# A four-direction selective scan between layer norm and FFN: padded middle-group weights, one load per quad of rows, other places for the pieces, and four products of a step on GpSimd

## The chip, the core and the metric

The kernel runs on one core of a Trainium2 chip. The metric is the device time of one execution in microseconds (us), the median of three runs. The engines of the core work side by side, each through its own instructions in order: TensorE (PE, matmuls; PEld is its weight load), VectorE (DVE), ScalarE (ACT), GpSimd (POOL), and SyncE (SP), whose queue issues the DMA transfers here. SBUF is the on-chip memory of 128 partitions, PSUM the memory that PE writes.

## What is computed

Two images of 96 channels and 128 x 128 pixels go through two layers. Layer 0 adds a state-space mixer (Mamba) over four scan directions to its input, then a quantized feed-forward network; layer 1 adds a 3 x 3 convolution and another feed-forward network. Nearly all the time goes into the mixer. Cut to what matters, for each direction:

```
xz = x @ in_w.T;  xc, z = split(xz)                 # 192 channels each
xc = silu(causal_conv_of_4_taps(xc) + conv_b)
dt_raw, B, C = split(xc @ xproj_w.T)                # 6, 16 and 16 columns
dt = softplus(dt_raw @ dt_w.T + dt_b)
for t in time:                                      # 16384 positions
    h = exp(dt[t] * A) * h + dt[t] * B[t] * xc[t]   # 192 channels x 16 states
    y[t] = sum over states of h * C[t]
out = (y + D * xc) * silu(z) @ outp_w.T
```

The four directions are row-major, its reverse, column-major and its reverse; their outputs are joined by one more matrix and added to the input.

## The kernel before

**Tiling.** For each image the kernel normalizes (`normalize`), runs the mixer (`mamba`), then the rest (`ffn_and_conv`). The mixer takes the directions in two pairs (`PAIRS`): row-major with column-major, then the two reverses. The 2 x 192 channels of a pair fill three groups (g) of 128 partitions: group 0 belongs to the first direction, group 2 to the second, and the middle group 1 has 64 channels of each, the first direction in partitions 0 to 63. Time is cut into 32 tiles of 512 positions; a pair and a tile make a *step*, 64 per image. A step has 24 *units*: a group and two of the 16 states (s, s + 1), so units 0 to 7 are group 0, 8 to 15 the middle group, 16 to 23 group 2.

**One unit.** ACT computes the two decays exp(dt * A) into a PSUM tile `da` (`decay`, L330; three buffers). POOL multiplies dt * u with the rows of B, in place in the row tile (`b_part`, L324). DVE runs two scans (`scan`, L334), which read da and b and leave the states h in da, and multiplies h with the rows of C into c (`behind`, L409, [128, 1024]). ACT saves the last states to `hst` (L410). PE adds the two halves of c into the PSUM tile `y` by identity matmuls (`sums`, L341); y starts with the D * xc term (`dmat`, L416). After the last unit of a group DVE multiplies y with the gate (`gated`, L349), and `project` and `collect` (L357, L359, L365) bring a step's groups into the image.

**Rows.** The rows of B and C of a step are computed on PE (L251), copied by ACT (`rows_out`, L258), written to DRAM four times over (`bcd`, L261), and read back with every partition getting the same 4 states x 512 positions (`row_tile`, L320). Such a *quad* serves two units. Groups 0 and 2 load it in one DMA of 1024 KB; the middle group, whose halves belong to two directions, takes two of 512 KB. B has four buffers of quads, C three.

**Order.** The order on PE, ACT, DVE, POOL and SP is the program's, written out by hand. The main loop over k, one unit each, issues: the B load of unit k + 6 (when k is even), `b_part` of unit k + 2, the pieces with (k, 0), the first scan of k, `behind(k - 1)`, the second scan of k, the C load of unit k + 4 (when k is even), the decay of k + 2, and the pieces with (k, 1). The *pieces* belong to the next step and are placed at units of the current one (`prologue`, its list `at`): the load of xa and xb, the input convolution of each group with its output copy (`conv`, `conv_out`), the gate (`gate`, `gate_out`), the silu of both (each with two loads of ACT's function table), the rows, and the softplus of dt in seven parts (`dt_in` to `dt_u`) for each group. All pieces share one PSUM bank, `misc`, so a piece's matmul waits until ACT has read the last one's result.

**What the change touches.** `inproj` (L197 to L208) writes the middle group as two matmuls of 64 columns each, one per direction, to the two halves of the bank. `BY_POOL` is empty in this kernel, so `by_pool` (L343) does not run: it would make a unit's product on POOL, with the states left in b.

Of the kernel before, what the change touches and what calls it, by code (L numbers as in the profile page):

```python
# [10 lines left out]
F32 = mybir.dt.float32  # L11
# [22 lines left out]
B_AHEAD = 3  # L34
C_AHEAD = 2
AHEAD = 2
BY_POOL = ()
BCO = 32
NBC = 4 * S

# [2 lines left out]
def tile_metaformer(ctx: ExitStack, tc: tile.TileContext, a: dict, out: bass.AP):  # L43
# [22 lines left out]
    inz = const("inz", (C, 4, DI))  # L66
# [11 lines left out]
    inx = cpool.tile([C, 4, 4, DI], F32, name="inx")  # L78
    nc.vector.memset(gmat, 0.0)
    with tc.tile_pool(name="prep", bufs=1) as pp, tc.tile_pool(name="prep_ps", bufs=2, space=PSUM) as pps:  # L80
        alog = pp.tile([128, 2, NG, S], F32, name="alog")
        nc.sync.dma_start(alog, a["alog"])
        nc.scalar.activation(alog, alog, AF.Exp)
        nc.vector.tensor_scalar_mul(amat, alog, -1.0)

        dskip = pp.tile([128, 2, NG], F32, name="dskip")
        nc.sync.dma_start(dskip, a["dskip"])
        for pi in range(2):
            for g in range(NG):
                nc.vector.tensor_scalar_mul(dmat[:, pi, g, :], ident, dskip[:, pi, g : g + 1])  # L90

        inxw = pp.tile([C, 4, DI], F32, name="inxw")
        nc.sync.dma_start(inxw, a["inx"])
        taps = pp.tile([C, 4, 4, DI], F32, name="taps")
        nc.sync.dma_start(taps, a["taps"].broadcast_to((C, 4, 4, DI)))
        for d in range(4):
            nc.vector.tensor_tensor(inx[:, d], taps[:, d], inxw[:, d, None, :].broadcast_to((C, 4, DI)), ALU.mult)
        outw = pp.tile([C, 4, DI], F32, name="outw")
        nc.sync.dma_start(outw, a["outw"])
        fusew = pp.tile([C, 4, C], F32, name="fusew")  # L100
        nc.sync.dma_start(fusew, a["fusew"])
        for pi, (da, db) in enumerate(PAIRS):

            pieces = [
                (slice(0, 128), da, 0, 128),
                (slice(0, 64), da, 128, 192),
                (slice(64, 128), db, 0, 64),
                (slice(0, 128), db, 64, 192),
            ]
            for g, (rows, d, lo, hi) in enumerate(pieces):  # L110
                ps = pps.tile([128, C], F32, name="ps")
                nc.tensor.matmul(ps[rows, :], outw[:, d, lo:hi], fusew[:, d, :], start=True, stop=True)
                nc.vector.tensor_copy(gmat[rows, pi, g, :], ps[rows, :])

    def layernorm(x, eps, dst, wp, psp, bufs=2, **cast):

# [66 lines left out]
    def mamba(acc, xnr, xnc):  # L183

        with ExitStack() as st:
# [8 lines left out]
            def misc():  # L194
                return ps_m.tile([128, T], F32, name="misc")

            def inproj(pi, g, w, src, taps):  # L197

                ps = misc()
                for k in taps:  # L200
                    se = {"start": k == taps[0], "stop": k == taps[-1]}
                    for d, rows, lo, hi in (
                        ((0, slice(0, 128), 0, 128),),
                        ((0, slice(0, 64), 128, 192), (1, slice(64, 128), 0, 64)),
                        ((1, slice(0, 128), 64, 192),),
                    )[g]:
                        nc.tensor.matmul(ps[rows, :], w(PAIRS[pi][d], k, lo, hi), src[d][:, k : k + T], **se)  # L207
                return ps  # L208

            def prologue(pi, i, d):  # L210
# [14 lines left out]
                    d["dt"], d["dtu"], d["yg"] = [], [], []  # L225

                def conv(g):
                    d["ps"] = inproj(pi, g, lambda dd, k, lo, hi: inx[:, dd, k, lo:hi], src, (0, 1, 2, 3))

                def conv_out(g):  # L230
                    if g == 0:
# [1 line left out]
                    nc.scalar.activation(d["xc"][:, g, :], d["ps"], AF.Identity, bias=convb[:, pi, g : g + 1])  # L233

                def gate(g):
                    d["ps"] = inproj(pi, g, lambda dd, k, lo, hi: inz[:, dd, lo:hi], src, (3,))

                def gate_out(g):
                    if g == 0:
# [13 lines left out]
                        )  # L253

                def rows_out():

                    d["rows"] = one.tile([BCO + NBC, T], F32, name="rows")
                    nc.scalar.copy(d["rows"], d["ps"][0 : BCO + NBC, :])  # L258
                    d["bcd"] = rows_d.tile([COPIES, 2, NBC // 2, T], F32, name="bcd")
                    for n in range(COPIES):  # L260
                        nc.sync.dma_start(d["bcd"][n].rearrange("k r t -> (k r) t"), d["rows"][BCO:, :])  # L261

# [35 lines left out]
                    d["dtu"].append(dtu)  # L298


                at = [(0, 0, load), (8, 1, partial(silu, "xc")), (14, 1, partial(silu, "sz"))]
                at += [(12, 0, rows), (12, 1, rows_out)]
                for g, k in enumerate((4, 5, 6)):
                    at += [(k, 0, partial(conv, g)), (k, 1, partial(conv_out, g))]
                for g, k in enumerate((7, 10, 11)):
                    at += [(k, 0, partial(gate, g)), (k, 1, partial(gate_out, g))]
                for g, k in enumerate((13, 18, 21)):
                    pieces = (0, 0, dt_in), (0, 1, dt_exp), (1, 1, dt_ln), (2, 0, dt_q), (3, 0, dt_log), (3, 0, dt_sum), (4, 0, dt_u)
                    at += [(k + m, where, partial(f, g)) for m, where, f in pieces]
# [12 lines left out]

            def b_part(d, g, b):
# [15 lines left out]
            def sums(s, y, c):  # L339
                for j in range(2):  # L340
                    nc.tensor.matmul(y, ident, c[:, j, :], start=False, stop=s + j == S - 1)  # L341
# [61 lines left out]
            def behind(k):  # L403

                n, u = divmod(k, nu)
                (pi, i), d, (g, s) = steps[n], state[n], units[u]
                h, c = hs.pop(k), cs.pop(k)
                if (g, s) not in BY_POOL:
                    nc.vector.tensor_tensor(c, h, c, ALU.mult)  # L409
                nc.scalar.copy(hst[:, g, s : s + 2], h[:, :, T - 1])  # L410
# [155 lines left out]
def _layout(v):  # L566

    f = np.float32
    order = [d for pair in PAIRS for d in pair]
    rows = lambda w: w[order].reshape(2, NG, 128, -1).transpose(2, 0, 1, 3)  # L570
# [11 lines left out]
    grouped = lambda w: w.reshape(2, NG, 128, -1).transpose(2, 0, 1, 3)  # L582
    out = {
        "x": v["x"].reshape(NB, C, L),
        "ident": np.eye(128, dtype=f),
        "inx": v["L0_conv_in_w"][:, :DI].transpose(2, 0, 1),
        "inz": v["L0_conv_in_w"][:, DI:].transpose(2, 0, 1),
        "taps": v["L0_conv_conv_w"].transpose(0, 2, 1)[None],
        "convb": rows(v["L0_conv_conv_b"])[..., 0],
        "bcw": grouped(bcw),  # L590
        "dtw": dtw,
        "dtb": rows(v["L0_conv_dt_b"])[..., 0],
        "alog": rows(v["L0_conv_A_log"]),
        "dskip": rows(v["L0_conv_Dp"])[..., 0],
        "outw": v["L0_conv_outp_w"].transpose(1, 0, 2),
        "fusew": v["L0_conv_fuse_w"].reshape(C, 4, C).transpose(2, 1, 0),
        "fuseb": v["L0_conv_fuse_b"].reshape(C, 1),
        "kw": v["L1_conv_kernel"].transpose(1, 2, 3, 0).reshape(C, 9, C),
# [24 lines left out]
```

## Time and profile before

| | us |
|---|---|
| median of 3 runs | 13006.98 |
| lowest, highest | 13003.53, 13008.28 |
| the profiled execution | 13004.29 |
| its span, first to last instruction | 13002.5 |

The page's columns for a group of instructions are: line, engine, operation, output and inputs, shape and number; then busy time in us and the mean of one in ns; then the idle time of the engine just before them and what ended it. A window's row gives its length, the busy time of each engine in it, PE's granted clock, the busy share of the DMA engines and what they moved. In the timeline a row is a start, a length, an engine, a line, an operation, and in brackets the idle time before it and its releaser.

The two mixers fill most of the span, the first from about 168 us to 5936 us, the second from about 6660 us to 12427 us (first scans and last gate products of the timeline). A 5200 us stretch inside the first, 600 to 5800 us, shows the shares there:

| engine | busy us of 5200 |
|---|---|
| DVE | 4946.10 |
| PE | 4358.69 |
| POOL | 4071.97 |
| ACT | 3502.99 |
| DMA share, GB/s | 0.92, 289 |

DMA issues: 2048 row loads of 1024 KB (7.5 us to landing), 2048 of 512 KB (8.0 us), 512 row writes of 128 KB (9.8 us).

### The profile page before, as it was taken

To read this page: it belongs to the slowest core of one execution; us is meant where nothing else is said; L and a number is where in the kernel's file an instruction comes from. 1 tells how busy PE (TensorE), PEld (TensorE's weight loads), DVE (VectorE), ACT (ScalarE), POOL (GpSimd) and SP (SyncE) were. 2 spreads that over 40 slices of the span, in tenths; PEclk is the share of its full clock that TensorE was granted. 3 is DMA by queue.
4 is the path that set the end of the run, shared out by engine and by line. 5 is a ranking of instruction groups with operands and counts; after the bars stand their busy time and mean duration, and the time that the engine had idled before them with its cause. 6 is when DMAs were issued, how large, how long until landed. Compare 5 with 4: busy or idle time off the path is not lost. (4 is left out here: it accounts for less than half of the span.)

```text
span 13002.5 us, 97992 instructions
## 1 busy us (share of the span) xinstructions
PE 10850.3 (83%) x24208; PEld 3987.1 (31%) x24208; DVE 11569.1 (89%) x10865; ACT 8560.0 (66%) x14738; POOL 9215.4 (71%) x4772
## 2 busy tenths in 40 slices
PE   6888888888888888888978888888888888888889
PEld 2323233333333333333323333332333333333233
DVE  5999999999999999995459999999999999999954
ACT  6666666666666666665566666666666666666655
POOL 4877778777787787772147778777787777877721
PEclk8999999999999999999989999999999999999999
DMA  7999999999999999992079999999999999999920
GB/s 226 287 294 282 298 288 285 295 283 298 288 285 295 283 295 289 285 295 68 13 226 285 298 283 292 290 285 298 285 291 291 284 298 286 290 294 281 296 61 13
DMA packets 545331, 3400.40 MB, mean 262 GB/s; under 512 B 81612, under 2 KB 82732, under 8 KB 146840
## 3 DMA queue, kind: packets, MB, share of 16 engines
q1 hardware_dynamic: 544760, 3394.12, 83.1%
q8 instruction: 195, 3.19, 0.1%
q14 instruction: 376, 3.08, 0.1%
HBM read 3288.94 MB, written 104.86 MB: 261 GB/s over the span
## 5 line engine op out<-in xcount | busy, mean ns | idle before, releaser
L324 POOL TENSOR_TENSOR row<-dtu,row 128x1024 f32<-128x1024 f32 x3072 | 7175.7, 2358 | 1739.3 <-DMA row<-bcd 1419.2
L334 DVE TENSOR_TENSOR_SCAN da<-da,hst,row 128x512 f32<-128x512 f32 x5952 | 7339.4, 1274 | 351.2 <-ACT da L330 194.6
L341 PE MATMUL y<-row,ident 128*128 128x512 f32 x12288 | 6120.1, 626 | 1113.3 <-DVE row L409 1098.9
L330 ACT ACTIVATE da<-dt,amat 128x512 f32<-128x512 f32 x6144 | 4249.4, 692 | 207.5 <-ACT hst L410 0.4
L341 PEld LDWEIGHTS y<-row,ident 128*128 128x128 f32 x12288 | 2288.9, 197 | 4779.4 <-DVE row L409 2292.3
L409 DVE TENSOR_TENSOR row<-da,row 128x1024 f32<-128x1024 f32 x3072 | 3705.9, 1206 | 19.6 <-DMA row<-bcd 18.8
L410 ACT COPY hst<-da 128x2 f32<-128x2 f32 x3072 | 484.0, 158 | 2235.5 <-DVE row L409 2233.3
L416 PE MATMUL y<-xc,dmat 128*128 128x512 f32 x768 | 526.1, 773 | 779.1 <-DVE sz L349 779.1
L287 POOL TENSOR_TENSOR q<-e,q 128x512 f32<-128x512 f32 x384 | 488.0, 1271 | 821.8 <-ACT hst L410 709.1
L233 ACT ACTIVATE xc<-misc,convb 128x512 f32<-128x512 f32 x384 | 264.2, 688 | 1117.5 <-PE misc L207 1117.5
L207 PE MATMUL misc<-xa,inx 96*128 96x512 f32 (+1 forms) x2048 | 932.4, 597 | 59.0 <-DMA xa<-xnr 57.2
L207 PE MATMUL misc<-xb,inx 96*64 96x512 f32 (+1 forms) x2048 | 928.1, 595 | 1.6 <-ACT xc L233 1.6
L531 POOL TENSOR_TENSOR acc<-acc,y 96x512 f32<-96x512 f32 x128 | 147.6, 1153 | 987.0 <-DVE y L530 987.0
L541 PE MATMUL pc<-pad,kw 96*96 96x512 f32 x1152 | 566.7, 593 | 0.0
L207 PEld LDWEIGHTS misc<-xa,inx 96*128 96x128 f32 (+1 forms) x2048 | 323.6, 163 | 625.5 <-issue 493.4
L293 POOL TENSOR_TENSOR dt<-dt,ln 128x512 f32<-128x512 f32 x384 | 486.9, 1268 | 30.1
L297 POOL TENSOR_TENSOR dtu<-dt,xc 128x512 f32<-128x512 f32 x384 | 488.5, 1272 | 0.5
L290 POOL TENSOR_TENSOR ln<-ln,q 128x512 f32<-128x512 f32 x384 | 488.1, 1271 | 0.5
L359 PE MATMUL misc<-sz,gmat 128*96 128x512 f32 x1024 | 483.6, 594 | 0.0
L416 PEld LDWEIGHTS y<-xc,dmat 128*128 128x128 f32 x768 | 129.0, 211 | 1102.1 <-DVE sz L349 1099.1
L268 PE MATMUL misc<-rows,dtw 12*128 12x512 f32 x768 | 439.7, 652 | 18.5 <-ACT dt L275 17.2
L132 DVE TENSOR_TENSOR xq<-xm,rs 96x512 fp8e5<-96x512 f32 x128 | 87.9, 687 | 387.8 <-ACT rs L128 387.8
(75 smaller groups left out, 8403.8 us busy)
## 6 DMA issues: line engine op xcount, KB each, us to landing
row<-bcd SPq DMA_DIRECT2D x2048, 1024.0 KB, 7.5
row<-bcd SPq DMA_DIRECT2D x2048, 512.0 KB, 8.0
bcd<-rows SPq DMA_DIRECT2D x512, 128.0 KB, 9.8
xa<-xnr SPq DMA_DIRECT2D x124, 193.1 KB, 5.8
xb<-xnc SPq DMA_DIRECT2D x124, 193.1 KB, 5.5
acc<-in_x_dram SPq DMA_DIRECT2D x16, 768.0 KB, 17.8
xnr<-xn SPq DMA_DIRECT2D x16, 768.0 KB, 4.3
xnc<-stg SPq DMA_DIRECT2D x16, 768.0 KB, 5.6
```

What stands on the lines that cost most here:

```text
L207: nc.tensor.matmul(ps[rows, :], w(PAIRS[pi][d], k, lo, hi), src[d][:, k : k + T], **se)
L287: nc.gpsimd.tensor_tensor(d["q"], d["e"], d["q"], ALU.subtract)
L290: nc.gpsimd.tensor_tensor(d["ln"], d["ln"], d["q"], ALU.add)
L293: nc.gpsimd.tensor_tensor(d["dt"][g], d["dt"][g], d["ln"], ALU.add)
L297: nc.gpsimd.tensor_tensor(dtu, d["dt"][g], d["xc"][:, g, :], ALU.mult)
L324: nc.gpsimd.tensor_tensor(b, d["dtu"][g][:, None, :].broadcast_to((128, 2, T)), b, ALU.mult)
L330: nc.scalar.activation(da[:, j, :], d["dt"][g], AF.Exp, scale=amat[:, pi, g, s + j : s + j + 1])
L334: nc.vector.tensor_tensor_scan(h[:, j, :], da[:, j, :], b[:, j, :], 0.0 if i == 0 else hst[:, g, s + j : s + j + 1], ALU.mult, ALU.add,)
L341: nc.tensor.matmul(y, ident, c[:, j, :], start=False, stop=s + j == S - 1)
L409: nc.vector.tensor_tensor(c, h, c, ALU.mult)
L416: nc.tensor.matmul(y, dmat[:, pi, g, :], d["xc"][:, g, :], start=True, stop=False)
L541: nc.tensor.matmul(pc, kw[:, t, :], rows, start=t == 0, stop=t == 8)
```

## The change

1. **Padded weights.** The in-projection's weights of the middle group are laid out on the host as two [96, 128] blocks, one per direction, with zeros in the other direction's columns. `inproj` adds them in one accumulation of 128 columns. The output weights are padded likewise.
2. **Rows in turn.** The middle group's channels of the two directions alternate by partition (the host permutes every array that has these channels), so its quad is one DMA of 1024 KB. The rows are written to DRAM by two DMAs, each with a broadcast source, in place of four.
3. **Pieces at other units**, and each output copy or dt part in the following half.
4. **Products on GpSimd.** Units with (g, s) = (0, 4), (0, 8), (1, 4), (1, 8), which are 2, 4, 10 and 12 of a step, have their states written over b and their product with C made on POOL; their sums on PE are issued two units later.
5. The taps' weights are prepared in four parts through one buffer.

```diff
-BY_POOL = ()
+BY_POOL = ((0, 4), (0, 8), (1, 4), (1, 8))
...
-            def inproj(pi, g, w, src, taps):
+            def inproj(g, w, src, taps):
 
                 ps = misc()
-                for k in taps:
-                    se = {"start": k == taps[0], "stop": k == taps[-1]}
-                    for d, rows, lo, hi in (
-                        ((0, slice(0, 128), 0, 128),),
-                        ((0, slice(0, 64), 128, 192), (1, slice(64, 128), 0, 64)),
-                        ((1, slice(0, 128), 64, 192),),
-                    )[g]:
-                        nc.tensor.matmul(ps[rows, :], w(PAIRS[pi][d], k, lo, hi), src[d][:, k : k + T], **se)
+                parts = [(k, j) for k in taps for j in ((0,), (1, 2), (3,))[g]]
+                for n, (k, j) in enumerate(parts):
+                    nc.tensor.matmul(ps, w(k, j), src[j // 2][:, k : k + T], start=n == 0, stop=n == len(parts) - 1)
                 return ps
...
                 def rows_out():
-
                     d["rows"] = one.tile([BCO + NBC, T], F32, name="rows")
                     nc.scalar.copy(d["rows"], d["ps"][0 : BCO + NBC, :])
-                    d["bcd"] = rows_d.tile([COPIES, 2, NBC // 2, T], F32, name="bcd")
-                    for n in range(COPIES):
-                        nc.sync.dma_start(d["bcd"][n].rearrange("k r t -> (k r) t"), d["rows"][BCO:, :])
+
+                def rows_to_dram():
+
+                    d["bcd"] = rows_d.tile([2, COPIES, NBC // 2, T], F32, name="bcd")
+                    for k in range(2):
+                        r = d["rows"][BCO + k * NBC // 2 : BCO + (k + 1) * NBC // 2, None, :]
+                        r = r.broadcast_to((NBC // 2, COPIES, T))
+                        nc.sync.dma_start(d["bcd"][k].rearrange("n r t -> r n t"), r)
...
-                at = [(0, 0, load), (8, 1, partial(silu, "xc")), (14, 1, partial(silu, "sz"))]
-                at += [(12, 0, rows), (12, 1, rows_out)]
-                for g, k in enumerate((4, 5, 6)):
-                    at += [(k, 0, partial(conv, g)), (k, 1, partial(conv_out, g))]
-                for g, k in enumerate((7, 10, 11)):
-                    at += [(k, 0, partial(gate, g)), (k, 1, partial(gate_out, g))]
-                for g, k in enumerate((13, 18, 21)):
-                    pieces = (0, 0, dt_in), (0, 1, dt_exp), (1, 1, dt_ln), (2, 0, dt_q), (3, 0, dt_log), (3, 0, dt_sum), (4, 0, dt_u)
+                at = [(0, 0, load), (7, 1, partial(silu, "xc")), (12, 1, partial(silu, "sz"))]
+                at += [(12, 1, rows), (13, 0, rows_out), (13, 1, rows_to_dram)]
+                for g, k in enumerate((2, 4, 6)):
+                    at += [(k, 0, partial(conv, g)), (k + 1, 0, partial(conv_out, g))]
+                for g, k in enumerate((9, 10, 11)):
+                    at += [(k, 1, partial(gate, g)), (k + 1, 0, partial(gate_out, g))]
+                for g, k in enumerate((14, 17, 20)):
+                    pieces = (0, 1, dt_in), (1, 0, dt_exp), (1, 1, dt_ln), (3, 0, dt_q), (4, 0, dt_log), (4, 0, dt_sum), (5, 0, dt_u)
                     at += [(k + m, where, partial(f, g)) for m, where, f in pieces]
...
                 t = gen.tile([128, 4, T], F32, name=f"row{k}", bufs=ahead + 1)
-                for half in range(2) if g == 1 else (slice(None),):
-                    rows = slice(half * 64, half * 64 + 64) if g == 1 else half
-                    at = s + S * (half if g == 1 else g // 2)
-                    n = (64 if g == 1 else 128) // COPIES
-                    src = d["bcd"][None, :, k, at : at + 4, :].broadcast_to((n, COPIES, 4, T))
-                    nc.sync.dma_start(t[rows], src)
+
+                rows, nd = d["bcd"][k].rearrange("n (d s) t -> n d s t", d=2)[:, :, s : s + 4, :], 2
+                if g != 1:
+                    rows, nd = rows[:, g // 2 : g // 2 + 1], 1
+                src = rows.rearrange("n d s t -> (n d) s t")[None].broadcast_to((128 // nd // COPIES, nd * COPIES, 4, T))
+                nc.sync.dma_start(t, src)
                 return t
...
-            def by_pool(s, y, h, c):
+            def by_pool(h, c):
                 nc.gpsimd.tensor_tensor(c, h, c, ALU.mult)
-                sums(s, y, c)
...
-                    later(k + 1, 1, by_pool, s, y, h, c)
+                    later(k + 1, 1, by_pool, h, c)
+                    later(k + 3, 1, sums, s, y, c)
...
-        taps = pp.tile([C, 4, 4, DI], F32, name="taps")
-        nc.sync.dma_start(taps, a["taps"].broadcast_to((C, 4, 4, DI)))
-        for d in range(4):
-            nc.vector.tensor_tensor(inx[:, d], taps[:, d], inxw[:, d, None, :].broadcast_to((C, 4, DI)), ALU.mult)
+        for k in range(4):
+            taps = pp.tile([C, 2, NG + 1, 128], F32, name="taps")
+            nc.sync.dma_start(taps, a["taps"][:, k].broadcast_to((C, 2, NG + 1, 128)))
+            nc.vector.tensor_tensor(inx[:, k], taps, inxw, ALU.mult)
...
+    def padded(w):
+
+        t = np.zeros((w.shape[0], 2, NG + 1, 128), f)
+        for pi, (p, q) in enumerate(PAIRS):
+            t[:, pi, 0] = w[:, p, :128]
+            t[:, pi, 1, 0::2] = w[:, p, 128:]
+            t[:, pi, 2, 1::2] = w[:, q, :64]
+            t[:, pi, 3] = w[:, q, 64:]
+        return t
```

`at` lists each piece as (unit, half, function); a piece with half 0 is issued before the unit's scans, with half 1 after the decay of unit k + 2. The load of xa and xb stays at unit 0.

More of the change, by code (lines that the diff above doesn't have):

```diff
@@ L65, in tile_metaformer @@
     nc.vector.tensor_scalar_add(center, ident[0:C, 0:C], -1.0 / C)
-    inz = const("inz", (C, 4, DI))
+    inz = const("inz", (C, 2, NG + 1, 128))
     convb = const("convb", (128, 2, NG))
@@ L77, in tile_metaformer @@
     gmat = cpool.tile([128, 2, NG + 1, C], F32, name="gmat")
-    inx = cpool.tile([C, 4, 4, DI], F32, name="inx")
-    nc.vector.memset(gmat, 0.0)
+    inx = cpool.tile([C, 4, 2, NG + 1, 128], F32, name="inx")
     with tc.tile_pool(name="prep", bufs=1) as pp, tc.tile_pool(name="prep_ps", bufs=2, space=PSUM) as pps:
@@ L90, in tile_metaformer @@
                 nc.vector.tensor_scalar_mul(dmat[:, pi, g, :], ident, dskip[:, pi, g : g + 1])
-        inxw = pp.tile([C, 4, DI], F32, name="inxw")
+        inxw = pp.tile([C, 2, NG + 1, 128], F32, name="inxw")
         nc.sync.dma_start(inxw, a["inx"])
-        taps = pp.tile([C, 4, 4, DI], F32, name="taps")
-        nc.sync.dma_start(taps, a["taps"].broadcast_to((C, 4, 4, DI)))
-        for d in range(4):
-            nc.vector.tensor_tensor(inx[:, d], taps[:, d], inxw[:, d, None, :].broadcast_to((C, 4, DI)), ALU.mult)
-        outw = pp.tile([C, 4, DI], F32, name="outw")
-        nc.sync.dma_start(outw, a["outw"])
+        for k in range(4):
+            taps = pp.tile([C, 2, NG + 1, 128], F32, name="taps")
+            nc.sync.dma_start(taps, a["taps"][:, k].broadcast_to((C, 2, NG + 1, 128)))
+            nc.vector.tensor_tensor(inx[:, k], taps, inxw, ALU.mult)
+        outx = pp.tile([C, 2, NG + 1, 128], F32, name="outx")
+        nc.sync.dma_start(outx, a["outx"])
         fusew = pp.tile([C, 4, C], F32, name="fusew")
         nc.sync.dma_start(fusew, a["fusew"])
[L102 to L110, printed above, removed]
+        for pi, pair in enumerate(PAIRS):
+            for g in range(NG + 1):
                 ps = pps.tile([128, C], F32, name="ps")
-                nc.tensor.matmul(ps[rows, :], outw[:, d, lo:hi], fusew[:, d, :], start=True, stop=True)
-                nc.vector.tensor_copy(gmat[rows, pi, g, :], ps[rows, :])
+                nc.tensor.matmul(ps, outx[:, pi, g, :], fusew[:, pair[g // 2], :], start=True, stop=True)
+                nc.vector.tensor_copy(gmat[:, pi, g, :], ps)
     def layernorm(x, eps, dst, wp, psp, bufs=2, **cast):
@@ L227, in conv @@
                 def conv(g):
-                    d["ps"] = inproj(pi, g, lambda dd, k, lo, hi: inx[:, dd, k, lo:hi], src, (0, 1, 2, 3))
+                    d["ps"] = inproj(g, lambda k, j: inx[:, k, pi, j, :], src, (0, 1, 2, 3))
                 def conv_out(g):
@@ L235, in gate @@
                 def gate(g):
-                    d["ps"] = inproj(pi, g, lambda dd, k, lo, hi: inz[:, dd, lo:hi], src, (3,))
+                    d["ps"] = inproj(g, lambda k, j: inz[:, pi, j, :], src, (3,))
                 def gate_out(g):
@@ L569, in _layout @@
     order = [d for pair in PAIRS for d in pair]
-    rows = lambda w: w[order].reshape(2, NG, 128, -1).transpose(2, 0, 1, 3)
+    perm = np.arange(2 * DI)
+    perm[128:256] = perm[128:256].reshape(2, 64).T.reshape(-1)
+    grouped = lambda w: w.reshape(2, NG, 128, -1).transpose(2, 0, 1, 3)
+    rows = lambda w: grouped(w[order].reshape(2, 2 * DI, -1)[:, perm])
     xw = v["L0_conv_xproj_w"]
@@ L581, in _layout @@
             dtw[k * RK : (k + 1) * RK, pi, at] = v["L0_conv_dt_w"][d].T
-    grouped = lambda w: w.reshape(2, NG, 128, -1).transpose(2, 0, 1, 3)
+    def padded(w):
[6 more added lines that the diff above has]
+        return t
     out = {
@@ L585, in _layout @@
         "ident": np.eye(128, dtype=f),
-        "inx": v["L0_conv_in_w"][:, :DI].transpose(2, 0, 1),
-        "inz": v["L0_conv_in_w"][:, DI:].transpose(2, 0, 1),
-        "taps": v["L0_conv_conv_w"].transpose(0, 2, 1)[None],
+        "inx": padded(v["L0_conv_in_w"][:, :DI].transpose(2, 0, 1)),
+        "inz": padded(v["L0_conv_in_w"][:, DI:].transpose(2, 0, 1)),
+        "taps": padded(v["L0_conv_conv_w"].transpose(2, 0, 1))[None],
         "convb": rows(v["L0_conv_conv_b"])[..., 0],
-        "bcw": grouped(bcw),
-        "dtw": dtw,
+        "bcw": grouped(bcw[:, perm]),
+        "dtw": dtw[:, :, perm],
         "dtb": rows(v["L0_conv_dt_b"])[..., 0],
@@ L594, in _layout @@
         "dskip": rows(v["L0_conv_Dp"])[..., 0],
-        "outw": v["L0_conv_outp_w"].transpose(1, 0, 2),
+        "outx": padded(v["L0_conv_outp_w"].transpose(1, 0, 2)),
         "fusew": v["L0_conv_fuse_w"].reshape(C, 4, C).transpose(2, 1, 0),
```

## The prediction

> **What bounds the kernel now.** I read the page's table of engines first, then the groups, then one step of the scan loop in the timeline of VectorE (DVE), TensorE (PE) and ScalarE (ACT), and last the windows cut at that step's three gate products.
>
> ```profile
> PE 10850.3 (83%) x24208; PEld 3987.1 (31%) x24208; DVE 11569.1 (89%) x10865; ACT 8560.0 (66%) x14738; POOL 9215.4 (71%) x4772
> L324 POOL TENSOR_TENSOR row<-dtu,row 128x1024 f32<-128x1024 f32 x3072 | 7175.7, 2358 | 1739.3 <-DMA row<-bcd 1419.2
> L334 DVE TENSOR_TENSOR_SCAN da<-da,hst,row 128x512 f32<-128x512 f32 x5952 | 7339.4, 1274 | 351.2 <-ACT da L330 194.6
> L409 DVE TENSOR_TENSOR row<-da,row 128x1024 f32<-128x1024 f32 x3072 | 3705.9, 1206 | 19.6 <-DMA row<-bcd 18.8
> ```
>
> DVE is the fullest, and of its three operations in a unit (two scans, one product with C) the product is a third. DVE stalls little on data: the DMA wait of POOL (1419 us) is slack of an engine that is not late.
>
> ```profile
> 2153.74:2185.25 31.51, 30.09 (x74) 11.66 (x74) 28.69 (x26) 16.94 (x31) 27.66 (x15) 1.00 0.89 230
> 2185.25:2215.14 29.89, 22.29 (x48) 7.57 (x48) 28.62 (x26) 24.11 (x38) 14.98 (x8) 1.00 1.01 321
> 2215.14:2243.63 28.49, 21.04 (x44) 7.44 (x44) 28.49 (x27) 19.90 (x37) 28.33 (x17) 1.00 0.86 330
> ```
>
> The columns are length, then busy time of PE, weight loads, DVE, ACT, POOL, then PE clock, DMA share, GB/s. A step is 24 units and lasts 89.89 us here, three thirds of 8 units. The last third is pure DVE work (28.49 of 28.49): 8 units of 3.49 us and a gate product of 0.59. The other two add 3.02 and 1.40 us of stall. In the first third PE is busy 30.09 of 31.51 us: there PE, not DVE, is the bound. What ends the stalls:
>
> ```profile
> 2170.19 0.64 PE L207 MATMUL misc<-xa,inx 96*64 96x512 f32 x1
> 2170.19 0.64 PE L207 MATMUL misc<-xb,inx 96*64 96x512 f32 x1
> 2170.67 0.59 PE L207 MATMUL misc<-xa,inx 96*64 96x512 f32 x1
> 2170.67 0.59 PE L207 MATMUL misc<-xb,inx 96*64 96x512 f32 x1
> ...
> 2175.60 3.60 PE L207 MATMUL misc<-xb,inx 96*128 96x512 f32 x8
> ```
>
> ```profile
> 2181.52 1.29 DVE L334 TENSOR_TENSOR_SCAN da<-da,hst,row 128x512 f32<-128x512 f32 x1 [1.50 <-ACT da L330]
> 2185.25 0.69 DVE L349 TENSOR_TENSOR sz<-y,sz 128x512 f32<-128x512 f32 x1 [1.33 <-PE y L341]
> 2212.81 1.29 DVE L334 TENSOR_TENSOR_SCAN da<-da,hst,row 128x512 f32<-128x512 f32 x1 [1.27 <-ACT hst L410]
> ```
>
> ```profile
> 2173.89 0.69 ACT L233 ACTIVATE xc<-misc,convb 128x512 f32<-128x512 f32 x1 [3.13 <-PE misc L207]
> ```
>
> See two things. The two 64-column matmuls of the middle group, one from xa and one from xb, start in the same instant: the pair costs one pitch (0.43 us), so the middle group's convolution takes 3.59 us, like the others. And ACT sits in order behind a convolution's result (3.13 us), with the decays of the coming units queued behind it.
>
> [...] L324 against L409, both 1024 elements, is 2358 / 1206 = 1.96. [...] here the first third, where half-tile loads run, moves 230 GB/s at share 0.89, the others 321 and 330. [...]
>
> **The change part by part**, per step, clock at 0 where unit 0's first scan starts (2147.95 in the window shown: unit 1's first scan at 2150.26 + 1.18, less 3.49).
>
> *Products to POOL.* Units 2, 4, 10, 12 lose their product on DVE. Product starts and the next scans lie 1.12 us apart, so DVE's own work falls by 4 x 1.12 = 4.5, from 85.5 (3 x 28.49) to 81.0 us. POOL gets 4 x 2.33 (two L324 take 4.67): 70.97 + 9.3 = 80.3. It fits only beside few waits; the pieces' extra unit between ln and q (POOL waits there for ACT, 7.03 us in this step) and the faster loads give it those. The scan writes SBUF instead of PSUM, which no row shows: at most 0.1 us each either way (hst and non-hst scans differ by 0.06), 0.4 a step in the part that counts; taken as 0.
>
> *Padded weights.* The middle group's convolution is now 16 matmul records of 128 columns in a row: 16 x 0.43 = 6.9 us instead of 3.59; its gate 1.72 instead of 0.9. PE per step: about 73.4 + 4.2 minus overlaps counted in the busy time, against 81 of DVE. It is not the bound over a step; it is in the first third.
>
> *Pieces at other units: the first third again.* PE in program order, from rows of the window: 6.5 the dmat matmul (after the gate product), 0.97 long; sums of unit 0 to 9.2; convolution of group 0, now in unit 2, to 12.65 (its xa was issued at 0.7 and lands in 5.8, in time); sums of unit 1 to 14.45; project of the previous step, 1.71 + 1.73, to 18.05; then no sums of unit 2 (moved two units on), so PE waits for ACT's collect, 1.06 us, to free the one misc bank: 19.25. Middle convolution to 26.15. Sums of 3 and 2 to 29.7, group 2's convolution to 33.2, sums of 5, 6, 4 and 7 to 40.1. Group 0's gate product can start then: 40.1 less its predecessor at 5.8 is 34.35 us, against 31.51.
>
> DVE's side of the same stretch: ACT has the decay of unit 6 behind the collect (done 20.8, wanted 19.3: 1.5 us), and of unit 7 behind the middle group's output at 26.2 (done 28.6, wanted 24.3: 4.3 us); then the gate product waits for PE 2.3 us. Unstalled DVE work in the third is 28.49 - 2.24 = 26.25; with 8.1 it is 34.35. So the saving of units 2 and 4 is lost here, and 2.85 more.
>
> *The second third.* 26.25 of DVE work. The silu of sz goes from unit 14 to 12: ACT has 4.08 (1.28 + 1.48 + 1.28), the rows copy 0.58 and a decay 1.4 behind the decay of unit 14, which waits for unit 11's product: unit 15's decay comes 1.3 us late, about today's 1.27. 27.55 against 29.89: 2.3 gained. PE has 22.3 + 0.9 + 0.9 in it, no bound.
>
> *The last third* is 28.49 before; the dt pieces lie one unit apart less but ACT keeps 0.8 us or more of lead: 0.
>
> *DMA and SP.* 2048 loads of 512 KB become 1024 of 1024 KB, four writes of the rows become two. DVE waits little for loads now, so I give it 0.2 us a step (all periods' mean is 90.1, the undisturbed one 89.9). Against it: the C buffer of a POOL unit is freed two units later, its sums being late; SP stands at that load and the B loads behind it. The C of unit 8 is issued at 29.8, lands (7.5) at 37.3 and is wanted at 37: hidden by the gate wait. The others have 1.5 to 3 us left.
>
> *Once only.* The taps come in four loads through one buffer, each with its product: about 5.7 + 0.4 + 0.9 = 7 us each, and the loads of x stand behind them on SP: 17 us (0 to 25).
>
> Sum: +2.85 - 2.3 - 0.2 = +0.35 us a step, x 128 = +45, +17: about 62 us on the profiled run's 13004.3 (span 13002.5). The median of the runs is 2.7 us above that run: 13,065.
>
> **Rivals.**
> A, faster: the longer middle convolution doesn't reach DVE. PE is late, but if the 16 records go at half the pitch I give them, or ACT's output does not stand before the decay of unit 7, the first third is 34.35 - 3.4 = 31.0 and the gain 0.55 + 2.3 + 0.2 = 3 us a step: 12,640; with no stall left at all it would be 81.0 + 1.3, 12,000. For it: PE is only 83% busy. Against: ACT waits on these outputs already, 1117.5 us over the run, and PE has 1.4 us free in that third.
> B, slower: C's buffers. If a load lands in 10 instead of 7.5 us (the range is 4.3 to 16.4), each of the three POOL-delayed C loads not hidden costs about 0.7 to 1 us: +2.2 a step on top of the forecast, 13,340. It decides from 9 us of landing time on.
> C, slower: POOL at 80.3 us with over 10 us of waits left is at 90.3 or more and paces DVE: with 12, 92.3, 13,300. Against: its DMA waits come from loads that get faster.
> D: the loads alone matter (the products gain nothing, PE hides): 13,007 - 25 = 12,980. It lies inside the forecast's range.
>
> **Numbers.** Forecast 0.52 (own range 12,900 to 13,230: 1.3 us a step of error, as a stall of either third can be off by one us); A 0.27; B 0.14; C 0.07. No change is within 0.2%, 26 us, which is what these runs can tell. From the forecast 0.10 lies faster, 0.12 within, 0.30 slower. Faster 0.37, same 0.12, slower 0.51. The range 12,640 to 13,300 leaves out A's lower half and B's tail, some 0.18.
>
> **What would show it.** Middle convolution: one run of 16 records, 6.9 us, with ACT's output waiting for it 5 us or more. DVE's largest stall at the decay of unit 7, some 4 us. Thirds near 34.4, 27.6, 28.5. POOL's DMA wait far below 1419 us. I am wrong if the first third is under 32 us (A), if DVE waits for DMA or POOL by more than 1 us a step (B, C), or if PE's pitch is not 0.43.

## The result

The changed kernel takes 13804.83 us (median of 4 runs, 13796.74 to 13816.01) against 13007.63 us: 1.0613 times the time before, 95% interval 1.0594 to 1.0631. The forecast was 13,065 us, the range 12,640 to 13,300. The direction was right and the size was wrong by 740 us.

The profiled execution's span is 13795.0 us against 13002.5. The page after, engines first and then the groups that answer to those shown of before:

```profile
PE 11354.6 (82%) x24208; PEld 4374.3 (32%) x24208; DVE 11104.7 (80%) x10352; ACT 8458.8 (61%) x14738; POOL 10406.0 (75%) x5284
L316 POOL TENSOR_TENSOR row<-dtu,row 128x1024 f32<-128x1024 f32 x3072 | 7182.8, 2355 | 2000.7 <-DMA row<-bcd 1513.2
L326 DVE TENSOR_TENSOR_SCAN da<-da,hst,row 128x512 f32<-128x512 f32 x4960 | 6199.1, 1281 | 809.8 <-ACT hst L401 605.9
L400 DVE TENSOR_TENSOR row<-da,row 128x1024 f32<-128x1024 f32 x2560 | 3105.1, 1213 | 650.1 <-DMA row<-bcd 648.0
L336 POOL TENSOR_TENSOR row<-row,row 128x1024 f32<-128x1024 f32 x512 | 1207.1, 2358 | 59.0 <-DMA row<-bcd 38.0
```

DVE has 464 us less to do and the span is 792.5 us longer. DVE's product waited 18.8 us for loads of C; it now waits 648.0. The idle time before its scans that leave the states in `da` rose from 351.2 to 809.8 us, 605.9 of them put down to ScalarE. The windows of one step, cut at its gate products (length; busy time of PE, weight loads, DVE, ACT, POOL; PE clock, DMA share, GB/s), show where:

```profile
2180.40:2214.62 34.22, 32.31 (x72) 13.35 (x72) 26.89 (x24) 17.65 (x30) 26.51 (x12) 1.00 0.72 184
2214.62:2247.70 33.08, 25.64 (x50) 9.70 (x50) 26.87 (x23) 23.66 (x42) 25.51 (x12) 0.90 0.98 275
2247.70:2276.18 28.48, 21.07 (x44) 7.44 (x44) 28.48 (x25) 18.77 (x35) 27.96 (x18) 1.00 0.97 376
```

Over all steps the medians of the thirds are 34.22, 33.12 and 28.48 us; predicted were 34.35, 27.55 and 28.49. The first and the last came as worked out. The second is 5.57 us too long, and 128 steps of that are 713 us: nearly the whole miss. DVE's stalls of over 1 us in these windows, from its timeline:

```profile
2203.07 1.29 DVE L326 TENSOR_TENSOR_SCAN da<-da,hst,row 128x512 f32<-128x512 f32 x1 [4.46 <-ACT hst L401]
2214.62 0.69 DVE L340 TENSOR_TENSOR sz<-y,sz 128x512 f32<-128x512 f32 x1 [1.94 <-PE y L333]
2230.82 1.23 DVE L400 TENSOR_TENSOR row<-da,row 128x1024 f32<-128x1024 f32 x1 [1.17 <-DMA row<-bcd]
2238.37 1.23 DVE L400 TENSOR_TENSOR row<-da,row 128x1024 f32<-128x1024 f32 x1 [3.45 <-DMA row<-bcd]
2247.70 0.69 DVE L340 TENSOR_TENSOR sz<-y,sz 128x512 f32<-128x512 f32 x1 [1.13 <-PE y L333]
```

The first two are the ones foretold in the first third (4.3 and 2.3 us). The two on L400, products of units 13 and 14 with C, were not. Where those loads were, in the trace's view of one line's DMA issues, here the six row loads issued from 2212.9 to 2223.4 us, and in the view of the DMA engines from 2216 to 2238 us (share in tenths and GB/s in 40 slices):

```profile
L312 SPq DMA_DIRECT2D row<-bcd x6: 514/522/541, 2212.9 to 2223.4; - x6
...
DMA to landing us min/median/max: 7.9/16.4/17.4
```

```profile
DMA  9889999999999987999999999999899999999998
GB/s 209 179 194 238 223 223 194 238 209 238 238 238 238 238 179 179 268 194 223 223 238 238 194 194 238 298 402 477 372 387 194 223 223 223 253 223 194 209 253 343
```

Six loads of 1 MB go out within 10.5 us and take up to 17.4 us to land. The DMA engines are full nearly all the time, at some 220 GB/s while the middle group's loads run and at 370 to 477 GB/s in the few slices of group 2's. So a middle load is still slow, though it is now one DMA to all 128 partitions.

For each load that was issued while the row load ahead of it was in flight I took the time between the two landings, as an estimate of what it occupies the engines for. Medians by group:

| kernel | groups 0, 2 | middle group |
|---|---|---|
| before | 3.00, 2.49 us | 2.34 us for each half, 4.69 for both |
| after | 3.01, 2.49 us | 4.72 us |

So the one load of 1 MB occupies the engines as long as the two halves that it replaces: the merge by itself saved no DMA time.

### The profile page after: what moved, and what is told of

The parts are those of the page before. It is cut to its first block, busy times and chain, and to the rows that moved or that the text cites. A ratio compares the mean times of both kernels' runs of the same rounds, so it can differ in the third digit from the quotient of the medians.

```text
span 13795.0 us, 96837 instructions
## 1 busy us (share of the span) xinstructions
PE 11354.6 (82%) x24208; PEld 4374.3 (32%) x24208; DVE 11104.7 (80%) x10352; ACT 8458.8 (61%) x14738; POOL 10406.0 (75%) x5284
## 3 DMA queue, kind: packets, MB, share of 16 engines
q14 instruction: 369, 3.01, 0.1%
## 5 line engine op out<-in xcount | busy, mean ns | idle before, releaser
L326 DVE TENSOR_TENSOR_SCAN da<-da,hst,row 128x512 f32<-128x512 f32 x4960 | 6199.1, 1281 | 809.8 <-ACT hst L401 605.9
L400 DVE TENSOR_TENSOR row<-da,row 128x1024 f32<-128x1024 f32 x2560 | 3105.1, 1213 | 650.1 <-DMA row<-bcd 648.0
L326 DVE TENSOR_TENSOR_SCAN row<-da,hst,row 128x512 f32<-128x512 f32 x992 | 1261.5, 1272 | 0.3 <-POOL row L316 0.3
L336 POOL TENSOR_TENSOR row<-row,row 128x1024 f32<-128x1024 f32 x512 | 1207.1, 2358 | 59.0 <-DMA row<-bcd 38.0
L195 PE MATMUL misc<-xa,inx 96*128 96x512 f32 x2048 | 1015.7, 608 | 204.1 <-ACT hst L401 138.7
L195 PE MATMUL misc<-xb,inx 96*128 96x512 f32 x2048 | 983.5, 592 | 1.6 <-ACT xc L221 1.6
L265 ACT ACTIVATE e<-misc,dtb 128x512 f32<-128x512 f32 x384 | 263.2, 685 | 660.7 <-PE misc L260 618.8
L195 PEld LDWEIGHTS misc<-xa,inx 96*128 96x128 f32 x2048 | 389.5, 195 | 776.6 <-issue 525.2
L195 PEld LDWEIGHTS misc<-xb,inx 96*128 96x128 f32 x2048 | 386.7, 189 | 494.6 <-issue 491.4
L340 DVE TENSOR_TENSOR sz<-y,sz 128x512 f32<-128x512 f32 x384 | 266.2, 693 | 329.8 <-PE y L333 329.2
L289 POOL TENSOR_TENSOR dtu<-dt,xc 128x512 f32<-128x512 f32 x384 | 488.5, 1272 | 0.5
```

What stands on the lines that cost most here:

```text
L195: nc.tensor.matmul(ps, w(k, j), src[j // 2][:, k : k + T], start=n == 0, stop=n == len(parts) - 1)
L289: nc.gpsimd.tensor_tensor(dtu, d["dt"][g], d["xc"][:, g, :], ALU.mult)
L326: nc.vector.tensor_tensor_scan(h[:, j, :], da[:, j, :], b[:, j, :], 0.0 if i == 0 else hst[:, g, s + j : s + j + 1], ALU.mult, ALU.add,)
```

## The experiments

Twelve kernels were run. "Thirds" are medians of the distances between gate products; "load waits" are what DVE waits for row loads in a step, over all steps. Runs 1, 4, 5, 11 and 12 are medians of four executions, the others single ones. The first set asks what makes the second third long.

**1. The source order of the middle load.** Two of the four copies are read, so the source repeats 32 times over 4 rows, not 16 times over 8:

```diff
                 if g != 1:
                     rows, nd = rows[:, g // 2 : g // 2 + 1], 1
-                src = rows.rearrange("n d s t -> (n d) s t")[None].broadcast_to((128 // nd // COPIES, nd * COPIES, 4, T))
+                else:
+                    rows = rows[0 : COPIES // 2]
+                src = rows.rearrange("n d s t -> (n d) s t")[None].broadcast_to((32, COPIES, 4, T))
```

> The changed kernel, but the middle group's load reads two of the four copies in DRAM, so that its source repeats 32 times over 4 rows, like the loads of the other groups, instead of 16 times over 8 rows. Theory 1 (the merged load itself is slow, 4.74 us per MB against 2.49, because of this order of its source, so the burst of six loads lands late): middle quads 2.5 us apart, DVE's waits for loads under 1 us a step, second third 27.6 to 29 us, 13,100 to 13,300 us in all. Theory 2 (the late sums of GpSimd's units hold C's buffers, so loads are issued too late whatever their rate): waits of 3 us a step or more stay, above 13,550. If the order of the source is not the cause of the rate, the quads stay at 4.7 us apart and the time at 13,800.

Measured: 13236.07 us, 1.0179 times before (1.0164 to 1.0194). Middle loads 2.50 us apart; load waits gone (5.1 us a step before this edit); thirds 34.20, 28.29, 29.54. DVE's group and the windows of one step:

```profile
L402 DVE TENSOR_TENSOR row<-da,row 128x1024 f32<-128x1024 f32 x2560 | 3092.6, 1208 | 0.1
```

```profile
2193.83:2228.03 34.20, 32.31 (x72) 13.35 (x72) 26.76 (x24) 17.64 (x30) 29.83 (x15) 1.00 0.47 184
2228.03:2256.32 28.29, 22.83 (x50) 8.69 (x50) 26.57 (x24) 22.37 (x39) 22.97 (x11) 1.00 0.85 334
2256.32:2285.86 29.54, 22.46 (x44) 7.81 (x44) 28.64 (x26) 19.76 (x37) 26.92 (x17) 0.94 0.88 351
```

Theory 1 holds for this wait: this one edit takes 561 us of the 792.5 off. The first third doesn't move. The last third is 1.06 us longer than in the changed kernel, 29.54 us against 28.48; DVE waits there 0.56 us a step for GpSimd's B products, which it does not in the changed kernel; the rest stays unexplained.

**2. No product on GpSimd** (`BY_POOL = ()` in the changed kernel).

> The changed kernel with no product on GpSimd. Theory 2: the waits for C go, under 0.5 us a step, although the middle quads still take 4.7 us; thirds near 34, 30 and 28.5, 13,300 us. Theory 1: loads are as slow, waits of 1 to 3 us a step stay, 13,400 to 13,650. If the products on GpSimd are what loses the time by another way (GpSimd itself late), it comes below 13,100.

Measured: 13583.74 us; load waits 2.5 us a step, thirds 33.45, 31.98, 28.48. So with the slow loads the four products cost about 220 us rather than save any, and half of the wait stays without them.

Theory 2 had it that GpSimd's late sums hold C's buffers. The traces show a second reason. Counted from unit 0's first scan, the load of C for unit 8 goes out at 22.3 us in the kernel before, at 29.7 in the changed one, and still at 28.5 in this one, which has no late sum (medians over the steps). Its buffer comes free with the sums of units 2 and 3 on TensorE. In the kernel before, both stand ahead of the middle convolution, which is at unit 5. The change moves that convolution to unit 4: in this run the sums of unit 3 stand behind it, in the changed kernel those of both units. First the kernel before, the four matmuls of unit 3's sums and then the load (in two halves); then this run, where the middle convolution comes ahead of the sums of units 3 and 4:

```profile
2168.38 1.88 PE L341 MATMUL y<-row,ident 128*128 128x512 f32 x4
2170.29 1.15 SPq L320 DMA_DIRECT2D row<-bcd  x2
```

```profile
2171.20 1.02 PE L195 MATMUL misc<-xa,inx 96*128 96x512 f32 x2
...
2178.07 3.60 PE L333 MATMUL y<-row,ident 128*128 128x512 f32 x8
2179.99 0.53 SPq L312 DMA_DIRECT2D row<-bcd  x1
```

**3. Sums of GpSimd's units earlier** (`later(k + 2, 0, sums, ...)` in place of `later(k + 3, 1, ...)`).

> The changed kernel with the sums of GpSimd's units issued one and a half units earlier, so that C's buffers come free earlier. Theory 2: DVE's waits for loads (5 us a step) fall by more than half, 13,250 to 13,500 us. Theory 1: they fall by less than a third, 13,600 or more.

Measured: 13789.17 us, load waits 4.7 us of 5.1; the first third is 35.89 us. This meets theory 1's number but tests neither theory: the load of C for unit 8 goes out at 31.4 us, not earlier than the 29.7 of the changed kernel, because the sums of unit 2 still stand behind the middle convolution. Whether freeing C's buffers earlier helps was not shown.

**4. The kernel before with the four products alone.**

```diff
-BY_POOL = ()
+BY_POOL = ((0, 4), (0, 8), (1, 4), (1, 8))
...
-                    later(k + 1, 1, by_pool, s, y, h, c)
+                    later(k + 1, 1, by_pool, h, c)
+                    later(k + 3, 1, sums, s, y, c)
```

> The kernel before with the products of units 2, 4, 10 and 12 on GpSimd and nothing else: half loads, paired 64-column matmuls and the old places of the pieces. The prediction's sums say: first third 31.5 to 32.7 (TensorE's chain without the longer convolution; the collect is no longer covered by the sums of unit 2), second 27.7, last 28.5, so 88 to 89 us a step and 12,740 to 12,860 us. Theory 2: C's buffers are held here too, and the waits for C bring it above 13,000.

Measured: 13445.66 us, 1.0345 times before (1.0324 to 1.0366), load waits 4.6 us a step, thirds 32.91, 31.87 and 28.49: my number was missed and theory 2's was met. The views of DVE's waits, this kernel's lines first and then before's:

```profile
DVE row L408 <- DMA row<-bcd: 589.9, 277, 6.4
DVE sz L348 <- PE y L341: 437.4, 237, 3.0
```

```profile
DVE sz L349 <- PE y L341: 171.0, 128, 2.1
```

The same slow half loads that cost DVE 18.8 us before now cost it 589.9. So the wait needs two things at once: a slow transfer, and loads that go out late for what DVE then asks of them. Take away the slow transfer (run 1), and it is gone; keep it, with C's buffers given back early and all products on DVE, and there is next to none (0.15 us a step in the kernel before, 0.2 in run 7). Late sums alone put the load of C for unit 8 at 27.5 us (this run), the other parts of the change without late sums at 28.5 (run 2), both together at 29.7. None of the kernels with slow middle loads has a second third under 29.88 us, the kernel before (29.89) included; with the fast load it is 28.29 in run 1 and 29.56 in run 10.

**5. Half loads in the new order** (the kernel before, half loads from two copies, 32 times over 2 rows).

> The kernel before, its middle half loads reading two of the four copies, so that each source repeats 32 times over 2 rows instead of 16 times over 4. If 64 partitions are what halves their rate[...], the half loads stay 2.3 us apart; if it is the order of the source, they come to about 1.25 us. VectorE waits for loads 0.15 us a step here, so the time stays within 0.3% of before either way.

Measured: 2.43 us a half, where 2.34 was; 13065.81 us, 1.0051 times before (1.0034 to 1.0067), just outside the 0.3% expected, with load waits of 0.9 us a step where 0.15 were. For half loads this order makes nothing faster: 512 KB in 2.43 us is 216 GB/s, and in the 2.34 us of before 224. That their 64 partitions are what holds them there was my guess; it fits these two figures, but no run shows it. The merged load goes to all 128 partitions, so the guess would not explain its 4.72 us.

**6. Eight copies**: groups 0 and 2 in the order that the middle group had (16 times over 8 rows), the middle group 32 times over 4.

> The rows written eight times; groups 0 and 2 load from all eight (source 16 times over 8 rows, the order that the changed kernel used for the middle group), the middle group 32 times over 4. If this order of the source is slow by itself, the loads of groups 0 and 2 go from 2.5 to 4.7 us each and the middle ones stay at 2.5; the time is then 13,400 us or more. If it was slow only for the middle group's alternating rows, all stay at 2.5 and the time at 13,240.

Measured: 16028.44 us. Groups 0 and 2 now take 4.63 us a load, the middle group 2.50. The share of 16 engines that the same row loads fill rises although the span is longer; the writes, eight copies now, add 67 MB (the queue's lines: packets, MB, share; run 1 first):

```profile
q1 hardware_dynamic: 524616, 3394.73, 67.6%
```

```profile
q1 hardware_dynamic: 557384, 3461.84, 82.6%
```

So it is the form of the source, not the group or its alternating rows. Two things change together in it, the repeats (16 or 32) and the rows per repeat (8 or 4, and so the bytes of DRAM that are read over and over); which one decides was not separated.

The second set asks about the first third.

**7. Padded weights alone** (the kernel before with two 128-column blocks for the middle group, not alternating).

```diff
-                for k in taps:
...
-                        nc.tensor.matmul(ps[rows, :], w(PAIRS[pi][d], k, lo, hi), src[d][:, k : k + T], **se)
+                parts = [(k, j) for k in taps for j in ((0,), (1, 2), (3,))[g]]
+                for n, (k, j) in enumerate(parts):
+                    nc.tensor.matmul(ps, w(k, j), src[j // 2][:, k : k + T], start=n == 0, stop=n == len(parts) - 1)
```

> The kernel before with the padded weights alone (blocks of 64 columns, not alternating; half loads, places and products as before). If the 16 records in a row cost what the prediction's sums say, the first third is 34 to 35 us instead of 31.5, and the time 13,350 to 13,600; if TensorE's slack hides them, 13,000 to 13,050.

Measured: 13379.81 us, thirds 34.59, 29.88, 28.49: 3.08 us more in the first third, none elsewhere. The weights alone cost 376 us of span.

**8. Half of the middle convolution left out** (run 1's kernel, the part from xb dropped in the middle group's convolution and gate).

> The changed kernel with the faster middle loads; it leaves out the second direction's half of the middle group's convolution and gate, so that these are 8 and 2 records instead of 16 and 4, as many as the paired ones took time for. If TensorE's chain is what sets the first third, it falls by about 3.4 us from 34.2 to 30.8, the other thirds stay, and the time is 12,780 to 12,860 us. If another wait stands behind it, the first third stays above 33.

Measured: 12862.19 us, with the work left out; first third 32.45 us in the median and 31.62 in the mean, the others as before it. 374 us come off where I expected 376 to 456. The third got 1.75 us shorter in the median and 2.64 in the mean, not the 3.4 us that the matmuls left out take: so TensorE's chain sets it at first, and something else takes over on the way; what, stays open.

**9. ScalarE's copy of the middle convolution a unit later** (run 1's kernel, `conv_out(1)` at unit 6).

> The changed kernel with the faster middle loads, and the middle convolution's output copy on ScalarE one unit later. If TensorE's chain bounds the first third, it stays at 33.5 to 34.5 us: VectorE's stall at the decay of unit 7 (4.35 us) falls below 1 us and its wait for TensorE at the gate product grows by as much; 13,180 to 13,260 us. If ScalarE's order is what costs, the first third falls to 30 or 31 us and the time to 12,850.

Measured: 13234.97 us, first third 34.19. The stall moved by one unit; it did not move to the gate product, as I had written: two lines of run 1's timeline of DVE, and two of this kernel's.

```profile
2216.48 1.29 DVE L328 TENSOR_TENSOR_SCAN da<-da,hst,row 128x512 f32<-128x512 f32 x1 [4.46 <-ACT hst L403]
2228.03 0.69 DVE L342 TENSOR_TENSOR sz<-y,sz 128x512 f32<-128x512 f32 x1 [2.17 <-PE y L335]
```

```profile
2221.91 1.29 DVE L328 TENSOR_TENSOR_SCAN da<-da,hst,row 128x512 f32<-128x512 f32 x1 [3.28 <-ACT da L324]
2226.49 0.69 DVE L342 TENSOR_TENSOR sz<-y,sz 128x512 f32<-128x512 f32 x1 [2.18 <-PE y L335]
```

Where DVE waits for ScalarE is a matter of ScalarE's order; how long the third lasts is not. Together with runs 7 and 8 this says that TensorE's chain sets it.

**10. Run 1's kernel without products on GpSimd.**

> The changed kernel with the faster middle loads and no product on GpSimd. The prediction's sums: first third 33.5 (TensorE's chain, so VectorE's two products there cost nothing), second 29.8 to 30, last 28.5, 13,200 to 13,260 us: the four products on GpSimd buy at most 30 us. If VectorE's work counted in full, it would be 4.5 us a step slower, 13,800.

Measured: 13241.83 us against 13236.07 with them; thirds 32.82, 29.56, 29.54. DVE's 4.5 us a step buy nothing that can be told: in the first third TensorE is the bound, and what units 10 and 12 save in the second (29.56 to 28.29) goes into the longer first third (32.82 to 34.20).

**11 and 12. Two tries at a faster version.** One is run 5's kernel with three products on GpSimd, all in the middle group (units 8, 10, 12):

> The kernel before with these half loads and with three products on GpSimd, all in the middle group (units 8, 10 and 12), where TensorE is not the bound. If the half loads got fast: thirds near 31.5, 27 and 28.5, 12,550 to 12,750 us, faster than both kernels. If they stay slow, the waits for C stay as in the kernel before with four products on GpSimd: 12,950 or more.

Measured: 13097.81 us, 1.0074 times before (1.0052 to 1.0097), load waits 3.6 us a step. The other is run 1's kernel with the pieces spread over the step, the middle convolution cut into two halves, and each `collect` one unit later (cut to the list of places):

```diff
+                at = [(0, 0, load), (12, 1, partial(silu, "xc")), (25, 1, partial(silu, "sz"))]
+                at += [(2, 0, partial(conv, 0)), (3, 0, partial(conv_out, 0))]
+                at += [(5, 0, partial(conv, 2)), (6, 1, partial(conv_out, 2))]
+                at += [(7, 0, partial(gate, 0)), (7, 1, partial(gate_out, 0))]
+                at += [(8, 1, partial(conv, 1, 0)), (9, 1, partial(conv, 1, 1)), (11, 1, partial(conv_out, 1))]
+                at += [(12, 0, partial(gate, 1)), (13, 1, partial(gate_out, 1))]
+                at += [(14, 0, partial(gate, 2)), (14, 1, partial(gate_out, 2))]
+                at += [(15, 0, rows), (15, 1, rows_out), (15, 1, rows_to_dram)]
+                for g, k in enumerate((16, 18, 20)):
```

> The changed kernel with the faster middle loads and the pieces spread so that no third has more of TensorE than it has of VectorE: the middle convolution in two halves at units 8 and 9, after group 0's sums, group 2's before it at unit 5, output copies behind the decay they used to hold up, the silu of the gate in the next step's first third. By the prediction's sums the thirds come to 27 to 28.5, 27.5 to 29 and 28.5 to 30: 12,250 to 12,650 us, faster than both kernels. If TensorE's load is not what stands in the way, no gain over 13,236.

Measured: 13517.44 us, 1.0395 times before (1.0377 to 1.0412), thirds 30.5, 31.27 and 33.11. The first third fell by 3.7 us, as TensorE's relief there should have it, and the other two grew by 6.6. DVE's waits moved with the pieces: in the second third it waits 2.75 us a step for TensorE at the gate product and 1.17 for decays (run 1: 1.84 us of waits in all), in the last 4.45 us for decays (run 1: 0.69 in all); its waits for GpSimd, 3.5 us, are in the first. I did not find which piece does it. No kernel of this study that does all the work beats the one before.

## Why the prediction was wrong, step by step

*TensorE's chain in the first third* was right. The middle convolution starts 19.1 us into the step (predicted 19.25) and takes 6.97 us (6.9), with ScalarE waiting 5.96 us for it, and the gate product starts at 40.0 (40.1). DVE's side of the sum agrees less well than its total: 7.33 us idle and 26.89 of work, where 8.1 and 26.25 were counted. The two come to the same total because TensorE sets the length. The timelines of PE and ACT:

```profile
2193.71 1.12 PE L195 MATMUL misc<-xa,inx 96*128 96x512 f32 x2 [1.12 <-ACT hst L401]
...
2200.68 3.60 PE L333 MATMUL y<-row,ident 128*128 128x512 f32 x8
```

```profile
2200.88 0.69 ACT L221 ACTIVATE xc<-misc,convb 128x512 f32<-128x512 f32 x1 [5.96 <-PE misc L195]
```

*Products to POOL*: right in their price (2358 ns each, scans into b 1272 ns against 1281 into da). That their saving is lost in the first third was right too; run 10 shows it, and that they make this third 1.4 us longer.

*The second third* was near as long as loads are fast: 27.55 predicted, 28.29 in run 1. *The last third* was right in the changed kernel (28.48 us); with fast loads it is 29.54.

*DMA and SP* is the step that failed, the sentences "The C of unit 8 is issued at 29.8, lands (7.5) at 37.3" and "The others have 1.5 to 3 us left". The issue times were right: in the step of the windows above, the C loads of units 8 and 10 went out 29.7 and 38.3 us after unit 0's first scan, where 29.8 was given and 38.3 follows from the sums of units 5, 6 and 4. Their reason was only half right: the sums of units 2 and 3 are late without GpSimd too, because the middle convolution was moved ahead of them (run 2). What was wrong is the landing. I took the median over the whole run before, 7.5 us, for loads that this same working put into a burst, and 16.1 us and 17.4 us were measured for those of units 12 and 14. Six loads that occupy the engines for 2.5 to 4.7 us each cannot all land 7.5 us after they were issued within 10.5 us: four middle loads of 4.7 us and two others of 2.5 add up to 24 us.

Behind that stands a second error: I counted on merged loads being faster, which was my estimate: the slow ones before were those to 64 partitions (2.34 us for 512 KB, where 1 MB of the other groups took 2.49 to 3.00), and I never asked whether that was their only difference. The merged load occupies 4.72 us, the two halves 4.69. And a sign of it was in the windows before: the DMA share of the second third was 1.01, the DMA engines were full in it, and I gave it 2.3 us off. With the fast load the share of that third is 0.85 (run 1).

With the source order alone corrected (run 1) the kernel takes 13236 us, inside the range and 171 us above the forecast. So the loads account for 569 us of the miss of 740; what remains lies mostly in the second and the last third. The forecast's own sum also has a slip of 4 us: 13004.3, 62 and 2.7 make 13,069.

Rival B had the mechanism (C's loads land late and DVE waits for them, deciding from 9 us of landing on), with chance 0.14 and a price of 2.2 us a step; the waits are 5.1 us, far over the 1 us named as the sign of being wrong. Rival C did not come: in the windows POOL is busy 79.98 of 95.78 us. In rival A the condition was false: the records go at 0.43 us.

*Once only*: nothing, not 17 us. The first gate product comes at 202.0 us (201.9 before), since loads of x were issued between those of the taps.

By size, in us of span: the padded weights alone +376 (run 7); the merged load in its order against the fast one +561 (run 1). The two overlap with what the other parts give back, so they are not to be added.

## What to carry to other kernels

When a change bunches transfers, sum what they occupy the DMA engines for, each at its own rate, instead of taking a median time to landing from a smoother schedule (7.5 us here, where 16.1 and 17.4 came). A load's rate can hang on the form of its source (4.72 us or 2.50 for the same 1 MB in the changed kernel and run 1): measure the gap between landings of loads in a queue, shape by shape, before counting on a merge to speed it up. Work taken from the fullest engine can be worth nothing in the stretches that another engine's chain, or full DMA engines, already set (13236.07 us with the four products on GpSimd, 13241.83 without, runs 1 and 10; with the slow loads, run 4, the second third even grew from 29.89 to 31.87 us); cut the step into windows first, and price each part. And when a piece moves ahead of others in an engine's order, ask which buffers those others were to give back.

## What was not expected of the hardware

One DMA of 1 MB to all 128 partitions ran at 222 GB/s (4.72 us) when its source repeated 16 times over 8 rows of 8 KB, and at 419 GB/s (2.50 us) when it repeated 32 times over 4 (run 1); in run 6 the groups' forms were the other way round, and groups 0 and 2 took 4.63 us, the middle group 2.50. Each packet of 8 KB is slower: in the changed kernel's DMA records the median one takes some 615 ns between the landings of two middle loads (the slow form) and 309 between those of two loads of the other groups (the fast one); in the kernel before it takes some 610 between two half loads. The engines were busy with both forms: in the changed kernel's windows their share is 0.98 at 275 GB/s in the second third and 0.97 at 376 in the last. Why one form is slower, these runs don't show.
